# Layer 3's bias table fetched by row gathers inside layer 1, and other orders, banks and buffers at three seams of a four-layer kernel

## The chip, the cores and the metric

The kernel runs on one core of a Trainium2 chip. The core has TensorE (PE in the profile), VectorE (DVE), ScalarE (ACT), GpSimd (POOL) and SyncE (SP), which here only issues DMAs. What counts is the time of one execution on the device in microseconds; several runs of the same program are taken, and the median is given. Every number type in the kernel is 32-bit float, apart from lists of indices.

## What is computed

Four residual layers work on an image batch `x` of shape 4 x 56 x 56 x 256. Each normalises `x` over 32 groups of channels and adds its own result to `x`:

```python
x = x + L0(_gn(x))   # attention of each pixel over its 7 x 7 neighbours, 8 heads of 32
x = x + L1(_gn(x))   # affinity of all 3136 tokens of an image with one another
x = x + L2(_gn(x))   # 7 x 7 neighbourhood attention with bias, dilation 1 and 2
x = x + L3(_gn(x))   # attention in shifted 7 x 7 windows, with bias table and mask
```

The bodies of layers 1 and 3, which the change touches most:

```python
# layer 1, n = 3136 tokens of an image
xn = x / norm(x)
A = exp(5.0 * (xn @ W_adj @ xn.T - rowmax));  A = A * (1 - eye);  A = A / rowsum(A)
diff = rowsum(A) * (x @ W_aff.T + b_aff) - (A @ x) @ W_aff.T
y = layernorm(diff) * gamma + beta;  y = where(y > 0, y, 0.01 * y)
# layer 3, windows of N = 49 tokens, 8 heads
bias = rel_bias_table[rel_index].reshape(N, N, HEADS).transpose(2, 0, 1)
attn = softmax(q @ k.T + bias + mask)      # mask: 0 or -100 by the window's place
out = (attn @ v) @ proj_weight.T + proj_bias
```

`rel_bias_table` has 169 rows of 8 numbers, one for each head; `rel_index` says which row belongs to each of the 49 x 49 pairs of a query and a key.

## The kernel before

The four layers follow one another in one program (`direct_blocks` with `layer0` to `layer3`). `run(l, layer, fixed, kinds)` opens the SBUF pools and the PSUM pool of a layer. In layers 0 and 2 a scheduler decides the order on all engines from the order in which the code gives its steps; in layer 1 the order of PE and DVE is that of the code, in layer 3 that of PE, DVE, ACT and POOL. A layer's stretch in the trace: layer 0 up to about 743 us, layer 1 to 2679, layer 2 to about 3332, layer 3 to the end at 3861.

PSUM tiles have tags. `ps_m` is the bank for projections and other small products (two buffers, in layer 1 one), `ps_s` holds scores, `ps_o` weighted sums, `ps_v` and `ps_t` belong to layer 1.

**The bias table** (`table_steps`, L1955 to L2007). Layer 3 needs for every pair of windows a table of bias plus mask, 98 keys x 8 heads x 98 queries, in four types. It is made inside layer 0's stream, three steps behind each row of attention. `look_up` (seven calls) takes seven queries: a cast of indices (L1974), two comparisons that make one-hot columns (L1977), four PE products with the table (L1981), copies (L1984), seven PE transposes (L1987) and a copy into `base` (L1988). `mask` (four calls) adds the mask's type to `base` (L1994, two halves), takes the exponential for half of the heads (L1996), and stores to the DRAM tensor `m3d` (L1998, eight stores in all). Layer 3 loads all of `m3d` in one piece, `m3l` of 2.46 MB.

**Layer 1** goes through (image, row tile j, range of columns) units. A unit makes scores `ps_s` from `xd` and `xnT` (L1440), exponentials on ACT (L1443), a product on POOL that clears the diagonal (L1445), transposes (L1531), and products into `ps_o` (L1545) and `ps_v` (L1550), of which DVE adds the latter to `acc` (L1472). `scaled(j)` makes `xd`, two POOL instructions (L1433), for a unit two ahead. `finish` makes y of a row tile (L1586 to L1609); its transposes and the addition to x are L1616 and L1624. While image b is worked on, `replace` puts the chunks of image b+1 in place, seven chunks of 512 tokens: token lengths (L1382), values (L1404, in two halves, evacuated by ACT L961 and DVE L959), and a product that spreads the reciprocal lengths (L1414) with which DVE makes `xnT` (L1416). These and L1616 all use `ps_m`, of which layer 1 has one bank.

**Layer 1 to 2.** Layer 2's first row was prepared inside layer 1. Its projections run values first (L979, evacuated by DVE L983), then queries and keys (L952, evacuated by ACT). DVE has layer 1's last tiles ahead of L983.

**Layer 2 to 3.** Layer 2's last additions (L1910) go into `xr` tiles (two buffers), loaded by SP (L1907) and stored by SP (L1913). Layer 3 begins with the values of two rows (L979, L983, stored to `vd` at L987 from one buffer `vt`), then row 0's projections (L952).

**Layer 3** has 32 rows r of 8 windows (four pairs) and two head halves hq, so 64 units (r, hq). `attend_quads` issues for each unit its scores (L1020), the exponentials and masks (L1024 to L1027), then `done` of the unit before (reciprocal L2109, product into `attn` L2111), the fill steps, which are projections of coming rows and the output projection of row r-2, and `products` of the unit before (L1035: first with v, then with ones for the sums). `project_out` multiplies `attn` with `w_p` (L952), adds the bias on ACT (L2131), adds to x on POOL (L2133) and stores. Behind the loop come the last `done`, `products`, `done` and the output projections of the last two rows. A short check of bounds (L2200 to L2208) ends the program.

## Time and profile before

| what | us |
|---|---|
| median of three runs | 3865.4 |
| lowest and highest of them | 3864.78, 3871.85 |
| the profiled execution | 3863.09 |
| its span in the profile | 3861.2 |
| PE without work in the span | 143 |

The rows of section 2 of the page, the span in 40 slices of 96.5 us, show how evenly the engines are used; a digit is the busy share in tenths, in the row PEclk the clock that PE was granted:

```profile
PE   7899999899999999999999999999999999899998
DVE  5676867633445444454444543445577777677775
POOL 3577777611124311242112421124677777555555
PEclk9899999899999999999999999999999999999998
```

The first eight slices are layer 0, the next twenty layer 1, in which PE has nearly all the work and the other engines little; then seven of layer 2 and five of layer 3. A row of the profile's groups gives line, engine, operation, output and input with their shapes and the count, then the busy time and the mean of one in ns, then the idle time of the engine ahead of it and what ended it. A line of the waits gives what an engine waited to do and for whom, with the total in us, the number and the longest. A row of the time line gives the start and the length in us.

### The profile page before, as it was taken

To read this page: it belongs to the slowest core of one execution; us is meant where nothing else is said; L and a number is where in the kernel's file an instruction comes from. 1 tells how busy PE (TensorE), PEld (TensorE's weight loads), DVE (VectorE), ACT (ScalarE), POOL (GpSimd) and SP (SyncE) were. 2 spreads that over 40 slices of the span, in tenths; PEclk is the share of its full clock that TensorE was granted. 3 is DMA by queue.
4 is the path that set the end of the run, shared out by engine and by line. 5 is a ranking of instruction groups with operands and counts; after the bars stand their busy time and mean duration, and the time that the engine had idled before them with its cause. 6 is when DMAs were issued, how large, how long until landed. Compare 5 with 4: busy or idle time off the path is not lost.

```text
span 3861.2 us, 112545 instructions
## 1 busy us (share of the span) xinstructions
PE 3717.8 (96%) x48953; PEld 2499.3 (65%) x48953; DVE 2219.1 (57%) x4232; ACT 1465.1 (38%) x3111; POOL 1761.9 (46%) x1924
## 2 busy tenths in 40 slices
PE   7899999899999999999999999999999999899998
PEld 4465656567777677776777767776666666455554
DVE  5676867633445444454444543445577777677775
ACT  4465656422222222222222222222666666344443
POOL 3577777611124311242112421124677777555555
PEclk9899999899999999999999999999999999999998
DMA  6544443400101000010000100001344444534443
GB/s 215 139 151 143 145 120 113 167 14 12 31 18 33 26 14 21 18 33 26 17 18 18 33 20 10 10 10 51 111 136 129 138 127 118 159 125 136 133 130 96
DMA packets 275650, 305.70 MB, mean 79 GB/s; under 512 B 31302, under 2 KB 266344, under 8 KB 274664
## 3 DMA queue, kind: packets, MB, share of 16 engines
q1 hardware_dynamic: 274858, 298.34, 25.5%
q8 instruction: 386, 6.32, 0.7%
q14 instruction: 118, 0.97, 0.1%
q10 hardware_dynamic: 288, 0.08, 0.0%
HBM read 205.95 MB, written 92.39 MB: 77 GB/s over the span
## 4 chain that ended last, share of the span: by engine, by line
PE 74%; DVE 3%; POOL 1%; issue 1%; ACT 1%; DMA 0%; SPq 0%; DVEq 0%; ACTq 0%; POOLq 0%
PE ps_o L1545 13%; PE ps_s L1440 13%; PE ps_m L952 13%; PE ps_v L1550 12%; PE ps_m L979 4%; PE ps_t L1531 3%; PE ps_o L1097 3%; PE ps_s L1068 3%; PE ps_o L1035 2%; PE ps_m L1404 2%; PE ps_s L1020 1%; PE ps_v L1511 1%; PE ps_o L1515 1%; PE ps_s L1482 1%; PE ps_m L1616 1%
## 5 line engine op out<-in xcount | busy, mean ns | idle before, releaser
L1472 DVE TENSOR_TENSOR acc<-acc,ps_v 128x257 f32<-128x257 f32 x1104 | 463.9, 423 | 785.0 <-PE ps_v L1550 756.4
L1550 PE MATMUL ps_v<-xw,e 128*128 128x257 f32 x2208 | 610.5, 381 | 1.8 <-DVE acc L1472 1.8
L1545 PE MATMUL ps_o<-xw,at 128*128 128x257 f32 x2208 | 609.0, 379 | 0.0
L1440 PE MATMUL ps_s<-xnT,xd 128*128 128x512 f32 (+3 forms) x1344 | 575.7, 551 | 3.9 <-DVE xnT L1416 3.9
L1534 ACT COPY at<-ps_t 128x512 f32<-128x512 f32 (+3 forms) x332 | 170.6, 514 | 957.1 <-PE ps_t L1531 956.9
L1550 PEld LDWEIGHTS ps_v<-xw,e 128*128 128x128 f32 x2208 | 414.2, 189 | 143.4 <-issue 84.1
L1088 POOL TENSOR_TENSOR b<-e 126x336 f32<-126x336 f32 (+5 forms) x512 | 496.9, 991 | 8.9 <-ACT e L1076 1.2
L1545 PEld LDWEIGHTS ps_o<-xw,at 128*128 128x128 f32 x2208 | 419.1, 190 | 60.1
L952 PE MATMUL ps_m<-xn,w_wqkv 128*32 128x392 f32 x4096 | 376.0, 496 | 13.1 <-DVE v L983 7.5
L1433 POOL TENSOR_SCALAR xd<-xnT,vec 128x128 f32<-128x128 f32 x192 | 116.3, 617 | 489.4 <-PE ps_s L1440 489.2
L1079 POOL TENSOR_TENSOR e<-e,m0t 126x672 f32<-126x672 f32 (+3 forms) x128 | 238.8, 1866 | 207.7 <-ACT e L1078 202.7
L1443 ACT ACTIVATE e<-ps_s 128x512 f32<-128x512 f32 x336 | 185.4, 552 | 374.7 <-PE ps_s L1440 367.7
L1440 PEld LDWEIGHTS ps_s<-xnT,xd 128*128 128x128 f32 x1344 | 226.7, 192 | 142.8 <-issue 127.7
L1079 POOL TENSOR_TENSOR e<-e,bias 119x784 f32<-119x784 f32 (+5 forms) x128 | 239.4, 1871 | 155.9 <-ACT e L1078 155.4
L1097 PEld LDWEIGHTS ps_o<-e,vp 124*32 124x32 f32 (+3 forms) x8192 | 199.3, 110 | 105.0 <-issue 82.8
L998 ACT ACTIVATE no<-rs 128x168 f32<-128x168 f32 (+2 forms) x256 | 93.9, 367 | 446.8 <-DVE rs L1875 191.5
L952 PEld LDWEIGHTS ps_m<-xn,w_wqkv 128*32 128x32 f32 x4096 | 123.5, 110 | 189.0 <-issue 129.1
L1875 DVE RECIPROCAL rs<-ps_o 128x196 f32<-128x196 f32 (+2 forms) x128 | 175.7, 1373 | 111.6 <-PE ps_o L1097 107.1
L1097 PE MATMUL ps_o<-e,vp 124*32 124x112 f32 (+3 forms) x8192 | 231.4, 248 | 5.3 <-POOL e L1079 4.6
L1076 ACT ACTIVATE e<-e 126x672 f32<-126x672 f32 (+5 forms) x256 | 219.7, 858 | 17.0 <-DVE e L1075 5.3
L1027 POOL TENSOR_TENSOR e<-e,m3l 98x784 f32<-98x784 f32 x64 | 119.6, 1869 | 205.8 <-ACT e L1024 205.8
L1078 ACT ACTIVATE e<-ps_s 126x672 f32<-126x672 f32 (+5 forms) x256 | 206.3, 806 | 9.1 <-PE ps_s L1068 9.1
(205 smaller groups left out, 6044.1 us busy)
## 6 DMA issues: line engine op xcount, KB each, us to landing
x<-xr SPq DMA_DIRECT2D x64, 392.0 KB
x<-in_x SPq DMA_DIRECT2D x53, 448.0 KB
x<-x SPq DMA_DIRECT2D x60, 392.0 KB
xr<-x SPq DMA_DIRECT2D x60, 392.0 KB
vd<-v SPq DMA_DIRECT2D x72, 256.0 KB
xr<-in_x SPq DMA_DIRECT2D x32, 392.0 KB
xr<-x SPq DMA_DIRECT2D x28, 448.0 KB
x<-xr SPq DMA_DIRECT2D x28, 448.0 KB
```

Source lines behind the costliest of these rows:

```text
L952: nc.tensor.matmul(pm[j * HD:(j + 1) * HD, :n], lhsT=w[:, h, col + j * HD:col + (j + 1) * HD], rhs=rhs(h), start=(h == 0), stop=(h == CC - 1))
L1076: nc.scalar.activation(ev, ev, AF.Exp)
L1078: nc.scalar.activation(ev, sv, AF.Exp)
L1079: nc.gpsimd.tensor_tensor(parts(ev), parts(ev), w["emask"], ALU.mult)
L1088: nc.gpsimd.tensor_tensor(w["b"][a][:nk, :, :2 * nq].rearrange("p h (i c) -> p h i c", i=2), ev[:, :, :, 0, :], ev[:, :, :, 1, :], ALU.add)
L1097: nc.tensor.matmul(w["o"](k, i)[j * HD:(j + 1) * HD], lhsT=ones[:nk, :HD] if k else v(j, u), rhs=w["b"][j // 2][:nk, j % 2, i * nq:(i + 1) ...
L1440: nc.tensor.matmul(s[:, :n], lhsT=xd[j][:, h, :], rhs=xnT[:, h, first * P:last * P], start=(h == 0), stop=(h == CC - 1))
L1443: nc.scalar.activation(e[:, :n], s[:, :n], AF.Exp, scale=5.0)
L1472: nc.vector.tensor_tensor(acc[:, i, :], acc[:, i, :], pv[:, :C + 1], ALU.add)
L1545: nc.tensor.matmul(out[j][:, :C + 1], lhsT=e[:, col(i)] if i == j else at[:, col(i)], rhs=xw[:, i, :], start=(i == j), stop=(i == NB - 1))
L1550: nc.tensor.matmul(pv[:, :C + 1], lhsT=e[:, col(i)], rhs=xw[:, j, :], start=True, stop=True)
L1875: nc.vector.reciprocal(rs.rearrange("p (t c) -> p t c", t=2), pv[:, :, 1, :])
```

## The change

1. The seven look-ups and four masks leave layer 0. In layer 1 a list of indices `idx` (98 rows, one for each of two times 49 keys; 49 columns, one for each query) is loaded, and behind each `scaled(j)` with 0 < j < 20 one gather is issued on POOL: for query q, 98 rows of the table, 8 floats each, to `rows`. Behind each seventh, SP stores them to the DRAM tensor `looked_up`. 49 gathers fall into the first three images.
2. Layer 2 loads `looked_up` and makes the four masks during its row 1 and later rows, at the last unit of a row in the code's order; the scheduler may put them earlier. The table's pools are opened in layer 2.
3. `replace` in layer 1 hands chunks 3, 4 and 5 a function `other_bank` that takes `ps_m` and `ps_v` in turn.
4. `mv` and `rstd` share one tile of the pool `late`.
5. Layer 2's row 0 projects queries, keys, values, in this order; `xr2` has three buffers in place of two; layer 1's late pool is closed earlier.
6. Layer 3: the table is loaded in two halves, `m3a` first and `m3b` behind the weights; `vt3` has two buffers and `xr3` three; two pools change places.
7. In `attend_quads` the sums come ahead of the values, and POOL's product is issued ahead of DVE's addition. The close of layer 3 is written out: products of the last units use `ps_m` banks, output projections the score banks, and the last row's projection is done in two halves of the input channels, the first while the reciprocal of the second is still being made; the bias goes into x by ACT, DVE adds from PSUM, and each half of the channels is stored by itself.

The diff, cut to its core:

```diff
@@ -944,9 +944,9 @@
-def project(w, col, rhs, n):
-    pm = ps_m()
+def project(w, col, rhs, n, pm=None):
+    pm = ps_m() if pm is None else pm
@@ -1011,7 +1011,7 @@
-    def logits(w):
+    def logits(w, between=no_step):
@@ -1022,13 +1022,14 @@
+        nc.gpsimd.tensor_tensor(ev[1], ev[1], w["emask"].to_broadcast([nk, 2, nu * nq]), ALU.mult)
+        between()
-        nc.gpsimd.tensor_tensor(ev[1], ev[1], w["emask"].to_broadcast([nk, 2, nu * nq]), ALU.mult)
-        for k in range(2):
+        for k in (1, 0):
@@ -1045,9 +1046,7 @@
-    done()
-    products(held)
-    held["done"]()
+    return logits, products, held, done
@@ -1295,10 +1294,6 @@
-                steps += table[:3]
-                if len(table) in (1, 2, 3):
-                    steps.append(tables.close)
-                del table[:3]
@@ -1316,9 +1311,6 @@
-    tables = ExitStack()
-    both = [tables.enter_context(tc.tile_pool(name=f"t{n}", bufs=n, side="right", reuse_waits="tile")) for n in (1, 2)]
-    table = table_steps(*both)
@@ -1329,6 +1321,10 @@
+m3d = dram.tile([98, 2, NH, 4, 98], FP, name="m3d")
+looked_up = dram.tile([98, WN, NH], FP, name="looked_up")
@@ -1344,6 +1340,20 @@
+    idx = big.tile([98, WN], I32, name="idx")
+    for w in range(2):
+        nc.sync.dma_start(out=idx[w * WN:(w + 1) * WN], in_=d["relidxT"])
+    def look_up(q):
+        if q % 7 == 0:
+            rows[:] = [pool.tile([98, 7, NH], FP, tag="rows", name="rows", bufs=1)]
+        with tc.issue_after(scaling[-1].ins):
+            nc.gpsimd.indirect_dma_start(out=rows[0][:, q % 7, :], out_offset=None, in_=d["table"][:, :],
+                                         in_offset=bass.IndirectOffsetOnAxis(ap=idx[:, q:q + 1], axis=0))
+        if q % 7 == 6:
+            nc.sync.dma_start(out=looked_up[:, q - 6:q + 1, :], in_=rows[0])
+    looks, scaling, rows = [lambda q=q: look_up(q) for q in range(WN)], [], []
@@ -1430,7 +1440,7 @@
-            nc.gpsimd.tensor_scalar_mul(xd[j][:, h, :], xnT[:, h, j * P:(j + 1) * P], adj[:, h:h + 1])
+            scaling.append(nc.gpsimd.tensor_scalar_mul(xd[j][:, h, :], xnT[:, h, j * P:(j + 1) * P], adj[:, h:h + 1]))
@@ -1593,11 +1603,11 @@
-        mv = pool.tile([P, 2], FP, tag="mv", name="mv1", bufs=7)
+        mv = late.tile([P, 3], FP, tag="mv", name="mv1", bufs=7)
-        rstd = pool.tile([P, 1], FP, tag="rstd", name="rstd", bufs=7)
+        rstd = mv[:, 2:3]
@@ -1688,11 +1698,16 @@
+    banks = iter(range(100))
+    def other_bank():
+        return psum_tile(*(("m", 1), ("v", 2))[next(banks) % 2])
-            (load,), normals[b, c], steps = tokens(b, c)
+            (load,), normals[b, c], steps = tokens(b, c, *([other_bank] if c in (3, 4, 5) else []))
@@ -1720,6 +1735,8 @@
+            if looks and 0 < units[k + 2][1] < 20:
+                looks.pop(0)()
@@ -1903,7 +1920,7 @@
-                box["x"] = pool.tile([P, CC, WC2], FP, tag="xr", name="xr2")
+                box["x"] = pool.tile([P, CC, WC2], FP, tag="xr", name="xr2", bufs=3)
@@ -1930,6 +1947,8 @@
+            if r and table:
+                work[7].append(table.pop(0))
@@ -1937,12 +1956,18 @@
-        for step in project_rows(i):
+        steps = project_rows(i)
+        for step in steps if i else steps[4:] + steps[2:4] + steps[:2]:
+    ends.close()
+    tables = ExitStack()
+    both = [tables.enter_context(tc.tile_pool(name=f"t{n}", bufs=n, side="right", reuse_waits="tile")) for n in (1, 2)]
+    table = table_steps(*both)
+    table.append(tables.close)
@@ -1950,54 +1975,25 @@
-    def look_up(q0):
...
+    found = big.tile([98, WN, NH], FP, name="found")
+    nc.sync.dma_start(out=found, in_=looked_up)
-            nc.vector.tensor_tensor(m[:, :, sl], base, t3[:, ty:ty + 1, sl].to_broadcast([98, NH, WN]), ALU.add)
+            nc.vector.tensor_tensor(m[:, :, sl], found.rearrange("p q h -> p h q"), t3[:, ty:ty + 1, sl].to_broadcast([98, NH, WN]), ALU.add)
-    return [lambda q=q: look_up(q) for q in range(0, WN, NQ)] + [lambda ty=ty: mask(ty) for ty in range(4)]
+    return [lambda ty=ty: mask(ty) for ty in range(4)]
@@ -2015,10 +2011,10 @@
-    def transfer(l, r, x, out):
+    def transfer(l, r, x, out, hs=slice(0, CC)):
-            ends = x[:, :, i0 * S:(i0 + n) * S], tokens_of(l, b, r0 * S, n * S)
+            ends = x[:, hs, i0 * S:(i0 + n) * S], tokens_of(l, b, r0 * S, n * S)[:, hs]
@@ -2029,10 +2025,12 @@
+    m3 = [big.tile([98, NH, 4 * 98], FP, name="m3a")]
+    nc.sync.dma_start(out=m3[0], in_=m3d[:, 0].rearrange("p h w k -> p h (w k)"))
-    m3 = big.tile([98, 2, NH, 4 * 98], FP, name="m3l")
-    nc.sync.dma_start(out=m3, in_=m3d.rearrange("p a h w k -> p a h (w k)"))
+    m3.append(pool.tile([98, NH, 4 * 98], FP, name="m3b", bufs=1))
+    nc.sync.dma_start(out=m3[1], in_=m3d[:, 1].rearrange("p h w k -> p h (w k)"))
@@ -2084,7 +2082,7 @@
-        v = pool.tile([P, 4, C], FP, tag="vt", name="vt3", bufs=1)
+        v = pool.tile([P, 4, C], FP, tag="vt", name="vt3", bufs=2)
@@ -2094,21 +2092,23 @@
-    def quad(r, hq):
+    def quad(r, hq, single=False):
-            if k + u == 0:
-                box["o"] = psum_tile("o", 1, 2)
-            return box["o"][:, k, u * 98:(u + 1) * 98]
+            if not box:
+                pair = None if single else psum_tile("o", 1, 2)
+                for i in (1, 0):
+                    box[i] = ps_m() if single else pair[:, i]
+            return box[k][:, u * 98:(u + 1) * 98]
-            nc.vector.reciprocal(rs, box["o"][:, 1, :WC])
+            nc.vector.reciprocal(rs, box[1][:, :WC])
-            nc.vector.scalar_tensor_tensor(attns[r][:, hq, :], box["o"][:, 0, :WC], 1.0, rs, ALU.mult, ALU.mult,
+            nc.vector.scalar_tensor_tensor(attns[r][:, hq, :], box[0][:, :WC], 1.0, rs, ALU.mult, ALU.mult,
@@ -2116,28 +2116,53 @@
-        mk = m3[:, wr // 7, 4 * hq:4 * hq + 4, :]
+        mk = m3[wr // 7][:, 4 * hq:4 * hq + 4, :]
-        x = pool.tile([P, CC, WC], FP, tag="xr", name="xr3")
+        x = pool.tile([P, CC, WC], FP, tag="xr", name="xr3", bufs=3)
-        def step(m):
-            pm = project(w_p, m * P, lambda h: attns[r][:, h, :], WC)
+        def step(m, pm=None):
+            pm = project(w_p, m * P, lambda h: attns[r][:, h, :], WC, pm)
-        return [lambda m=m: step(m) for m in range(CC)]
+        return [lambda *pm, m=m: step(m, *pm) for m in range(CC)]
+    def last_row(r):
+        x = pool.tile([P, CC, WC], FP, tag="xr", name="xr3", bufs=3)
+        transfer(3, r, x, 0)
+        pms = []
+        def first():
+            pair = psum_tile("o", 1, 2)
+            for m in range(CC):
+                pms.append(pair[:, m, :WC])
+                half(m, 0)
+                nc.scalar.activation(x[:, m, :], x[:, m, :], AF.Identity, bias=bp3[:, m:m + 1])
+        def half(m, h):
+            for j in range(4):
+                nc.tensor.matmul(pms[m][j * HD:(j + 1) * HD], lhsT=w_p[:, h, m * P + j * HD:m * P + (j + 1) * HD],
+                                 rhs=attns[r][:, h, :], start=(h == 0), stop=(h == CC - 1))
+        def second():
+            for m in range(CC):
+                half(m, 1)
+                for w, xv in parts(pms[m], x[:, m, :]):
+                    nc.vector.tensor_tensor(xv, xv, w, ALU.add)
+                transfer(4, r, x, 1, slice(m, m + 1))
+        return first, second
-        for r in range(n):
+        for r in range(n - 1):
@@ -2147,7 +2172,7 @@
-                w = quad(r, hq)
+                w = quad(r, hq, single=(r == n - 2 and hq == 1))
@@ -2159,10 +2184,27 @@
-    attend_quads(pool, stream())
-    for r in range(NIMG * 8 - 2, NIMG * 8):
-        for step in project_out(r):
-            step()
+    logits, products, held, done = attend_quads(pool, stream())
+    r = NIMG * 8 - 1
+    attns[r] = pool.tile([P, CC, WC], FP, tag="attn", name="attn3", bufs=3)
+    u3, u4 = quad(r, 0), quad(r, 1, single=True)
+    out = project_out(r - 2)
+    logits(u3, done)
+    out[0]()
+    products(held)
+    logits(u4, held["done"])
+    products(u3)
+    pair = psum_tile("s1", 1, 2)
+    out[1](pair[:, 0])
+    out = project_out(r - 1)
+    first, second = last_row(r)
+    out[0](pair[:, 1])
+    u3["done"]()
+    products(u4)
+    out[1](psum_tile("s0", 1, 2)[:, 0])
+    u4["done"]()
+    first()
+    second()
@@ -2188,7 +2230,7 @@
-run(3, lambda own: layer3(*own), {E.PE, E.DVE, E.Activation, E.Pool}, range(4))
+run(3, lambda own: layer3(own[1], own[0], *own[2:]), {E.PE, E.DVE, E.Activation, E.Pool}, (1, 0, 2, 3))
@@ -2254,6 +2296,7 @@
+g["relidxT"] = f(np.asarray(i["L3_conv_rel_index"]).reshape(WN, WN).T)
```

More of the change, by code (lines that the diff above doesn't have):

```diff
@@ L1595, in finish @@
             st = pool.tile([P, 6], FP, tag="st", name="st1")
-            mv = pool.tile([P, 2], FP, tag="mv", name="mv1", bufs=7)
+            mv = late.tile([P, 3], FP, tag="mv", name="mv1", bufs=7)
             nc.vector.bn_stats(out=st[:n], in_=y)
-            nc.vector.bn_aggr(out=mv[:n], in_=st[:n])
+            nc.vector.bn_aggr(out=mv[:n, :2], in_=st[:n])
             nc.vector.tensor_scalar_add(mv[:n, 1:2], mv[:n, 1:2], LN_EPS)
-            rstd = pool.tile([P, 1], FP, tag="rstd", name="rstd", bufs=7)
+            rstd = mv[:, 2:3]
             nc.gpsimd.tensor_tensor(rstd[:n], mv[:n, 1:2], mhalf[:n, 0:1], ALU.pow)
@@ L1948, in layer2 @@
             step()
-    m3d = dram.tile([98, 2, NH, 4, 98], FP, name="m3d")
     def table_steps(big, pool):
-        NR, NQ = 169, 7
-        idx = big.tile([P, WN, WN], I32, name="idx")
-        nc.sync.dma_start(out=idx.rearrange("p a b -> p (a b)"), in_=d["relidx"].to_broadcast([P, WN * WN]))
-        row = big.tile([P, 2], I32, name="row")
-        nc.gpsimd.iota(row, pattern=[[P, 2]], base=0, channel_multiplier=1)
-        rowf = big.tile([P, 2], FP, name="rowf")
-        nc.vector.tensor_copy(rowf, row)
-        tab = big.tile([P, 2, NH], FP, name="tab")
-        nc.sync.dma_start(out=tab[:, 0], in_=d["table"][:P])
-        nc.sync.dma_start(out=tab[:NR - P, 1], in_=d["table"][P:])
         t3 = big.tile([98, 4, 98], FP, name="t3")
         nc.sync.dma_start(out=t3, in_=d["c_m3"])
-        base = big.tile([98, NH, WN], FP, name="base")
-        def look_up(q0):
-            idxf = pool.tile([P, NQ, WN], FP, tag="idxf", name="idxf")
-            nc.vector.tensor_copy(idxf, idx[:, q0:q0 + NQ, :])
-            hot = pool.tile([P, 2, NQ * WN], FP, tag="hot", name="hot")
-            for a, n in ((0, P), (1, NR - P)):
-                nc.vector.tensor_scalar(hot[:n, a, :], idxf[:n].rearrange("p q k -> p (q k)"),
-                                        rowf[:n, a:a + 1], None, ALU.is_equal)
-            pb = ps_m()
-            for a, n in ((0, P), (1, NR - P)):
-                nc.tensor.matmul(pb[:NH, :NQ * WN], lhsT=tab[:n, a, :], rhs=hot[:n, a, :], start=(a == 0), stop=(a == 1))
-            tb = pool.tile([NH, NQ, 98], FP, tag="tb", name="tb")
-            for w in range(2):
-                nc.vector.tensor_copy(tb[:, :, w * WN:(w + 1) * WN], pb[:NH, :NQ * WN].rearrange("p (q k) -> p q k", k=WN))
-            pt = ps_m()
-            for q in range(NQ):
-                nc.tensor.transpose(pt[:98, q * NH:(q + 1) * NH], tb[:, q, :], ident[:NH, :NH])
-            nc.vector.tensor_copy(base[:, :, q0:q0 + NQ], pt[:98, :NQ * NH].rearrange("p (q h) -> p h q", h=NH))
+        found = big.tile([98, WN, NH], FP, name="found")
+        nc.sync.dma_start(out=found, in_=looked_up)
         def mask(ty):
```

## The prediction

> **What bounds the kernel now.** I read the page's head and its chain of waits first, then TensorE's waits, then the time line at each place that the change touches.
>
> ```profile
> span 3861.2 us, 112545 instructions
> PE   3717.8 (96%) x48953; PEld 2499.3 (65%) x48953; DVE 2219.1 (57%) x4232; ACT 1465.1 (38%) x3111; POOL 1761.9 (46%) x1924
> PE 74%; DVE 3%; POOL 1%; issue 1%; ACT 1%; DMA 0%; SPq 0%; DVEq 0%; ACTq 0%; POOLq 0%
> ```
>
> TensorE (PE) is busy for 96% of the span and carries the chain; the next engine stands at 57%. Time can be won in three ways only: PE work taken out, PE waits taken out, low-clock stretches avoided. Span minus PE busy is 143 us. The waits (engine, what waited, for whom: total us, times, longest) that lie where the change works:
>
> ```profile
> PE ps_o L1035 <- DVE attn L2111: 9.5, 6, 3.5
> PE ps_m L952 <- DVE v L983: 7.9, 4, 6.9
> PE ps_m L1616 <- DVE xnT L1416: 7.8, 3, 2.6
> PE ps_m L1987 <- DVE tb L1984: 7.5, 4, 3.0
> PE ps_m L979 <- DVE xr L1910: 5.9, 1, 5.9
> PE ps_m L1414 <- DVE xw L959: 2.6, 3, 0.9
> PE ps_m L952 <- DVE vt L983: 2.1, 1, 2.1
> PE ps_m L1404 <- ACT xw L961: 2.0, 3, 0.7
> ```
>
> In order: the close of layer 3, the door from layer 1 to layer 2, layer 1's change of image (three changes: 1616, 1414, 1404), the table look-ups, and the door from layer 2 to layer 3. Together 45 us, nearly a third of all that PE idles.
>
> [...] 32 matmuls of L1035 take 0.89 us at 3821.83 and 1.53 us at 3828.62, behind a wait of 2.90 us. So a wait costs more than its own length.
> [...]
>
> **The change part by part.**
>
> **Layer 0: 7 look-ups and 4 masks leave.** PE's groups in the stretch 60 to 190 us, and the DVE waits between, are all here:
>
> ```profile
> L1981 PE MATMUL ps_m<-hot,tab 128*8 128x343 f32 (+1 forms) x28 | 13.8, 603 | 0.0
> L1987 PE MATMUL ps_m<-ident,tb 8*98 8x8 f32 x49 | 4.3, 208 | 7.5 <-DVE tb L1984 7.5
> ```
>
> 13.8 + 4.3 = 18.1 us of PE work and 7.5 us of waiting: 25.6. Nothing but PE is full there (from 60 to 260 us PE 183.9 of 200, DVE 143, POOL 121, ACT 100), and DVE loses 28 us too (L1977 12.0 by two forms, L1984 6.4, L1994 5.2, L1974 2.9, L1988 1.3). Layer 0 is ordered by the scheduler, and its waits for ACT and DVE may come a little more often once PE catches up: I take 24, bounds 20 to 28 (the clock is granted at 0.91 there, so a little more is possible).
>
> **Layer 1: 49 gathers on POOL.** Each follows a pair of L1433 (2 x 0.617 us). 19 per image, in three images. POOL sat idle 489 us ahead of the 192 L1433, and in the stretch that I looked at 4.94 us between a pair and the next POOL work, the mask L1445 that PE needs next. [...] Behind it in POOL's queue stand L1445, L1586 and the pow L1601. Lower bound 0 (no PE work goes away); upper bound, where a gather outlasts its 4.94 us now and then, 49 x 0.3 = 15. The 7 stores of 22 KB go by SP, nobody waits for them in this layer but the next seventh gather, one tile being used.
>
> **Layer 1: two banks in turn for chunks 3 to 5.** With one ps_m bank the next user waits until the last is evacuated. Alternating with ps_v, L1616 no longer stands behind L1414/L1416 (2.61), values1 not behind the evacuation L961 (0.68), L1414 not behind L959 (0.88): 4.2 per image change, 12.5 for three. The 1.31 of L1440 stays, it needs xnT itself; so does 0.52 for L1624. Against it: ps_v is what L1550 rotates through, and a bank held for an evacuation of 0.6 to 0.7 us can delay an L1550 (0.5 per image, about 1.5). Take 11; bounds 3 (the waits only change bank) and 18 (the four L1440 at 1316.61 took 3.53 instead of 1.88 us, low clock, and that goes as well).
>
> **Layer 1 to 2: row 0's projections run queries, keys, values.**
>
> ```profile
> 2679.53 2.80 PE L979 MATMUL ps_m<-w_wqkv,xn 128*32 128x256 f32 x48
> 2689.18 7.01 PE L952 MATMUL ps_m<-xn,w_wqkv 128*32 128x392 f32 x64 [6.85 <-DVE v L983]
> ```
>
> L983 stands on DVE behind the tail of layer 1's y (L1604, L1609) and comes only at 2688.45. The four L952 groups need ACT alone, which is free by 2683.5, so their 7.01 us fill the hole, then 2.80 of L979, and L983 comes at about 2690.2: a wait of some 0.9 is left. Take 6; bounds 4 and 7.
>
> **Masks at layer 2's head.** 8 L1994 of 0.697 us now read the gathered rows with a stride, 4 exponentials, 8 stores (2.5 MB), and loads of t3, the rows and m3a (1.23 MB) on SP. About half falls into 5.5 us in which DVE is idle at 2712; the rest delays a L1075 or L983 by up to 1.2 us each. Take -2; bounds 0 and -4 (a strided read is in no trace; twice 0.697 is the upper end I allow).
>
> **Layer 2 to 3.**
>
> ```profile
> 3336.94 1.16 DVE L1910 SCALAR_TENSOR_TENSOR xr<-ps_m,vec,xr 128x392 f32<-128x392 f32 x2 [5.77 <-issue]
> 3338.15 8.18 PE L979 MATMUL ps_m<-w_wqkv,xn 128*32 128x256 f32 x96 [5.89 <-DVE xr L1910]
> 3348.43 3.83 PE L952 MATMUL ps_m<-xn,w_wqkv 128*32 128x392 f32 x44 [2.10 <-DVE vt L983]
> ```
>
> DVE waits for the last xr, which SP asks for at 3330.71, behind the store that frees its buffer and in the wake of the 2.46 MB table load issued at 3322.65. Three buffers let it load a row earlier, half of the table is in place since layer 2, and two vt buffers take the 2.10 (L983 waited for the store of vt). The 96 L979 should take 5.6 us (32 take 1.91) and took 8.18: 2.6 of low clock go too. 5.89 + 2.10 + 2.6 = 10.6; a rest of about 1.5 stays. Take 9; bounds 6 and 11. The other half of the table now loads beside the v gather: late by up to 8 us it harms nobody.
>
> **Steady layer 3.** Sums before values, POOL's multiply issued before DVE's add, other tile homes: PE is busy 472 of 473 us from 3350 to 3823. Cost 0.
>
> **The close of layer 3.** From 3823.3 PE works, waits 2.90, 2.22 and 3.47 us for L2111, and runs half of its work at low clock; last, 64 L952 (two rows of projection):
>
> ```profile
> 3828.62 1.53 PE L1035 MATMUL ps_o<-e,v 98*32 98x98 f32 x32 [2.90 <-DVE attn L2111]
> 3837.89 0.89 PE L1035 MATMUL ps_o<-e,v 98*32 98x98 f32 x32 [2.22 <-DVE attn L2111]
> 3843.42 1.53 PE L1035 MATMUL ps_o<-e,v 98*32 98x98 f32 x32 [3.47 <-DVE attn L2111]
> 3846.00 6.96 PE L952 MATMUL ps_m<-attn,w_wp 128*32 128x392 f32 x64
> ```
>
> Laying out the new order with full-clock durations (L1020 0.95, L1035 0.87 a half, L952 1.52 a half, L2109 2.60, L2111 0.57): scores of (31,0) end at 3824.2, DVE has (30,0) by 3826.5 and adds its mask by 3827.5, scores of (31,1) end 3828.5, products of (31,0) 3830.2, projections fill to 3833.2, products of (31,1) run 3833.2 to 3835.0, one more projection, L2109 and L2111 for (31,1) end at 3838.1 while PE does the early half of the last projection, the late half is done at 3839.7, the last DVE add about 3841, against 3855.1 for the last L2133 now. That is 14. The check at the end (L2200 to L2208) now stands behind the last adds instead of beside them, and 7.1 us lay between it and the end of the span: 3 us go back. Take 11; bounds 5 (PE waits again for reciprocals, low clock) and 14.
>
> **Sum.** 24 + 11 + 6 - 2 + 9 + 11 = 59. The profiled execution took 3863.1 us (span 3861.2), 2.3 below the median of 3865.4; 3863.1 - 59 = 3804, and on the median's footing 3806. All good ends: 28 + 18 + 7 + 11 + 14 = 78, 3787. All bad ends: 20 + 3 + 4 - 4 + 6 + 5 = 34, 3831, or 3846 with gathers at 15.
>
> **Rivals.**
> - Layer 0 isn't set by PE where the look-ups stood: L1068 waits for L1075 and L952 for kE already (7.8 and 7.6 us), so its neighbours inherit the time and 24 becomes 5: 3825. For it: the look-ups were placed by a scheduler that could fill holes. Against: the look-ups caused waits themselves, no engine but PE is above 72% there.
> - The bank swap only shifts the waits to L1550, and the close goes on waiting for reciprocals: 11 and 11 become 3 and 5: 3820.
> - Slower: the gathers hold POOL. Everything else brings 59, so they must cost 49 x 1.36 us or more on PE's path to be slower by 0.2%. With 4.94 us of cover a gather would have to hold POOL about 6.3 us[...]; at 8 us it would be 49 x 3.06 = 150 lost, 3896. For it: nothing in the trace shows such a DMA[...]. Against: POOL's idle time is wide.
>
> **How the numbers follow.** This kernel's measurement tells 0.2% (7.7 us) from no change. Chances: forecast 0.64 (3788 to 3816), layer 0 not set by PE 0.14, swap and close moved only 0.13, gathers slower 0.06, gains just eaten up 0.03. 8 in 10 lie from 3788 to 3832. Faster 0.91, same 0.03, slower 0.06.
>
> **What would show it.** L1987's wait gone and layer 0 ending near 718 instead of 743; at each image change only 1.31 and 0.52 left; no wait over 2 us at the first L979 of layer 2 or at layer 3's start; the stretch from 3823 to the end about 11 us shorter; POOL's gathers each under 5 us and no new wait of PE for e or xd in layer 1. Wrong: L1440 or L1545 waiting for POOL, L1550 for L1472 for longer, layer 0's L1068 and L1097 waits up by over 10 us, or layer 2's first 60 us longer.

## The result and the profile after

The changed kernel takes 3800.4 us in the median of six runs (3789.3 to 3803.0), against 3865.4 us for the kernel before (six runs): a ratio of 0.9823, with a 95% interval of 0.9807 to 0.984. That is 65 us less, 6 us below the forecast of 3806 and inside its range. The sum was right; four of its terms were not, two too small and two too large.

The page of the changed kernel, its head and its chain of waits (the profiled execution took 3789.3 us, the shortest of the six):

```profile
span 3787.5 us, 112437 instructions
PE 3672.9 (97%) x48876; PEld 2486.9 (66%) x48876; DVE 2201.7 (58%) x4195; ACT 1463.2 (39%) x3111; POOL 1811.6 (48%) x1966
PE 87%; DVE 7%; POOL 2%; ACT 2%; issue 1%; DMA 1%; SPq 0%; DVEq 0%; ACTq 0%; POOLq 0%
```

PE is busy 44.9 us less (3717.8 to 3672.9) and idle 28.8 us less. Only 18.1 us of PE work left the program. So some 27 us of the busy time that vanished, an estimate from these two numbers, are the same matmuls at a higher clock (the mean granted over the span rose from 0.985 to 0.994): this is the first thing that the prediction undervalued. POOL is 50 us busier: the gathers.

PE's waits in the changed kernel (what waited, for whom: total us, times, longest). Line numbers of layer 1 are up by ten, L1075 is now L1074, L1035 is L1036:

```profile
PE ps_s L1067 <- DVE e L1074: 12.8, 13, 2.4
PE ps_s L1450 <- DVE xnT L1426: 3.9, 3, 1.3
PE ps_m L1036 <- ACT pr L2131: 2.6, 1, 2.6
PE ps_o L2152 <- DVE xr L2159: 2.6, 1, 2.6
PE ps_m L979 <- DVE v L983: 2.4, 1, 2.4
PE ps_v L1560 <- DVE xnT L1426: 2.2, 3, 0.7
PE ps_m L952 <- ACT kE L1828: 1.4, 1, 1.4
PE ps_m L979 <- DVE vt L983: 0.6, 1, 0.6
```

Of the eight waits shown before, the largest of L1035, L1616, L1987, L979 for xr, L1414 and L1404 are gone; the 6.9 us for the values (v) shrank to 2.4 us, the 2.1 us for vt to 0.6 us. The 3.9 us of L1450 stay as foreseen. New are: 5.2 us in the close (L1036 for L2131, L2152 for L2159), the 2.4 us of L1067 and the 1.4 us for kE in layer 2's head, and, over the three image changes, 2.2 us of L1560 and 2.3 us more of L1626 waiting for xr (3.8 us in place of 1.5).

To see where the time went, the span is cut at seven matmuls that both kernels have: the first product with ones of layer 1, the first with `xdr`, layer 2's first projection, the first statistics in layer 2 (L914), its last product (L1097), layer 3's first scores (L1020), and the scores of unit (31,0). A second execution of the changed kernel (from the experiments) stands beside the first:

| stretch | before | after | after, again | forecast of the difference |
|---|---|---|---|---|
| layer 0 | 744.4 | 703.3 | 706.0 | -24 |
| start of layer 1 | 53.0 | 48.9 | 53.4 | 0 |
| rest of layer 1 | 1882.2 | 1866.6 | 1866.6 | -11 |
| layer 2, head | 53.8 | 56.6 | 57.5 | -4 (order -6, masks +2) |
| layer 2, rest | 592.3 | 592.6 | 594.2 | 0 |
| layer 2 to 3 | 28.2 | 18.0 | 18.0 | -9 |
| layer 3 | 469.5 | 469.7 | 469.7 | 0 |
| close, to the span's end | 37.9 | 31.7 | 31.2 | -11 |
| span | 3861.2 | 3787.5 | 3796.6 | -59 |

The differences of the first execution add up to -73.7, those of the second to -64.6. Between the two executions, 4.5 us lie in the start of layer 1, where the order is the same, and the rest in layers 0 and 2; the start of layer 1 took 53.0 us before and 53.4 us in the second execution, so its 4 us in the first are no effect of the change. They are the clock: it was granted at 0.90 in this stretch of the first execution and at 0.82 in the second, as in the kernel before (0.82), while PE was idle for 4.5 us in all three. The times of whole runs show the same: the two short ones of the six (3789.3 and 3789.9 us) have a mean granted clock of 0.994 and 0.995, the other four (3799.0 to 3803.0 us) of 0.991 and 0.992.

**Layer 2's head** is the stretch that went the wrong way. DVE in the changed kernel, from the time line (start, length, operation, idle time ahead of it and what ended it):

```profile
2647.84 3.21 DVE L1990 TENSOR_TENSOR m<-found,t 98x392 f32<-98x392 f32 x4 [0.73 <-DMA found<-looked_up]
...
2661.91 1.62 DVE L1990 TENSOR_TENSOR m<-found,t 98x392 f32<-98x392 f32 x2 [4.71 <-DMA m3d<-m]
2663.45 0.96 DVE L1074 TENSOR_TENSOR e<-ps_s,bias 85x784 f32<-85x784 f32 x1
```

and PE at the same place:

```profile
2664.47 1.96 PE L1067 MATMUL ps_s<-q,kI 32*90 32x84 f32 x32 [2.38 <-DVE e L1074]
2666.36 2.84 PE L952 MATMUL ps_m<-xn,w_wqkv 128*32 128x392 f32 x16
2668.97 1.53 PE L1096 MATMUL ps_o<-e,vp 85*32 85x98 f32 x32
```

The masks have two buffers. The third mask's addition waits until the first mask is stored, and DVE stands for 4.71 us with the scores' addition L1074 behind it in its queue. PE waits 2.38 us for that addition, and what follows runs at half clock (granted from 2664.4 to 2671.2 us). The same three groups in the kernel before:

```profile
2725.03 0.88 PE L1068 MATMUL ps_s<-q,kI 32*90 32x84 f32 x32
2725.84 1.52 PE L952 MATMUL ps_m<-xn,w_wqkv 128*32 128x392 f32 x16
2727.18 0.86 PE L1097 MATMUL ps_o<-e,vp 85*32 85x98 f32 x32
```

Wait and low clock make 2.38 + 1.08 + 1.32 + 0.67 = 5.5 us that go back to buffers that were missing.

**The close.** PE in the changed kernel:

```profile
3761.49 0.89 PE L1036 MATMUL ps_m<-e,v 98*32 98x98 f32 x32 [2.64 <-ACT pr L2131]
...
3766.86 1.52 PE L952 MATMUL ps_s<-attn,w_wp 128*32 128x392 f32 x16 [0.79 <-ACT pr L2131]
...
3776.01 0.86 PE L2152 MATMUL ps_o<-attn,w_wp 128*32 128x392 f32 x8 [2.60 <-DVE xr L2159]
```

The reciprocals are no longer waited for. In their place PE waits for ACT's evacuation and for DVE's last addition, and the clock holds (0.86 to 0.89 for a half of L1036). From the scores of (31,0) to the end of the span PE is idle for 16.6 us in both kernels; its busy time for the same matmuls fell from 21.2 to 15.1 us. So what the new close gained is clock, not idle time. At the very end, from the matmul of the check (n_safe) to the end of the span, 9.65 us pass, before 7.45.

### The profile page after: what moved, and what is told of

Its sections match the earlier page's. It is cut to its first block, busy times and chain, and to the rows that moved or that the text cites. A ratio compares the mean times of both kernels' runs of the same rounds, so it can differ in the third digit from the quotient of the medians.

```text
span 3787.5 us, 112437 instructions
## 1 busy us (share of the span) xinstructions
PE 3672.9 (97%) x48876; PEld 2486.9 (66%) x48876; DVE 2201.7 (58%) x4195; ACT 1463.2 (39%) x3111; POOL 1811.6 (48%) x1966
## 4 chain that ended last, share of the span: by engine, by line
PE 87%; DVE 7%; POOL 2%; ACT 2%; issue 1%; DMA 1%; SPq 0%; DVEq 0%; ACTq 0%; POOLq 0%
PE ps_m L952 17%; PE ps_o L1555 14%; PE ps_s L1450 13%; PE ps_v L1560 13%; PE ps_m L979 7%; PE ps_o L1096 5%; PE ps_s L1067 5%; PE ps_t L1541 3%; PE ps_o L1036 2%; PE ps_s L1020 1%; PE ps_m L1414 1%; POOL b L1087 1%; DVE e L1074 1%; DVE rs L1247 1%; PE ps_v L1521 1%
## 5 line engine op out<-in xcount | busy, mean ns | idle before, releaser
L1560 PE MATMUL ps_v<-xw,e 128*128 128x257 f32 x2208 | 611.3, 381 | 3.4 <-DVE xnT L1426 2.2
L1555 PE MATMUL ps_o<-xw,at 128*128 128x257 f32 x2208 | 609.2, 380 | 0.0
L1450 PE MATMUL ps_s<-xnT,xd 128*128 128x512 f32 (+3 forms) x1344 | 571.6, 548 | 3.9 <-DVE xnT L1426 3.9
L1560 PEld LDWEIGHTS ps_v<-xw,e 128*128 128x128 f32 x2208 | 414.4, 190 | 143.6 <-issue 83.1
L1555 PEld LDWEIGHTS ps_o<-xw,at 128*128 128x128 f32 x2208 | 419.9, 190 | 59.2
L952 PE MATMUL ps_m<-xn,w_wqkv 128*32 128x392 f32 x4096 | 376.2, 496 | 6.0 <-ACT gst L917 3.9
L1450 PEld LDWEIGHTS ps_s<-xnT,xd 128*128 128x128 f32 x1344 | 225.8, 191 | 141.1 <-issue 126.0
L952 PEld LDWEIGHTS ps_m<-xn,w_wqkv 128*32 128x32 f32 x4096 | 124.4, 110 | 180.0 <-issue 128.1
L1075 ACT ACTIVATE e<-e 126x672 f32<-126x672 f32 (+5 forms) x256 | 219.6, 858 | 13.3 <-DVE e L1074 1.1
L979 PE MATMUL ps_m<-w_wqkv,xn 128*32 128x256 f32 x3136 | 197.8, 383 | 3.1 <-DVE v L983 2.4
```

What stands on the lines that cost most here:

```text
L952: nc.tensor.matmul(pm[j * HD:(j + 1) * HD, :n], lhsT=w[:, h, col + j * HD:col + (j + 1) * HD], rhs=rhs(h), start=(h == 0), stop=(h == CC - 1))
L979: nc.tensor.matmul(pm[i:i + HD, j * C:(j + 1) * C], lhsT=xn[:, h, first + i:first + i + HD], rhs=w[:, h, :], start=(h == 0), stop=(h == CC ...
L1075: nc.scalar.activation(ev, ev, AF.Exp)
L1450: nc.tensor.matmul(s[:, :n], lhsT=xd[j][:, h, :], rhs=xnT[:, h, first * P:last * P], start=(h == 0), stop=(h == CC - 1))
L1555: nc.tensor.matmul(out[j][:, :C + 1], lhsT=e[:, col(i)] if i == j else at[:, col(i)], rhs=xw[:, i, :], start=(i == j), stop=(i == NB - 1))
L1560: nc.tensor.matmul(pv[:, :C + 1], lhsT=e[:, col(i)], rhs=xw[:, j, :], start=True, stop=True)
```

## The experiments

Twelve runs were made. A median is of four runs in the same round as the kernel before, unless a single run is named; for the stretches the landmarks of the table above are used.

### The changed kernel once more

> The changed kernel once more, for the spread between executions and as the measure for the other three. Theory 1 (the gain of layer 0 beyond its PE work and its wait is the clock that the waits behind the look-ups had taken away): layer 0 again lasts about 703 us and its clock from 60 to 200 us is granted at 0.98 or more; where this execution is 10 us longer than the profiled one of the changed kernel (3787.5), the difference lies in stretches of low clock at the starts of layers and not in any wait of fixed place. Rival (the gain of layer 0 is a lucky execution): layer 0 lasts 710 us or more.

Median 3804.4 us (3798.4 to 3807.4), ratio 0.9842 (0.9825 to 0.9858); layer 0 706.0 us. So the gain of layer 0 is no lucky execution: in ten executions of kernels with this layer 0, these and the ones below, it lasted 703.2 to 707.8 us. The spread lies in stretches of low clock that come or don't: the start of layer 1 takes 48.5 to 50.6 us or 52.3 to 53.7 us, whatever the kernel, and the close as it was changed takes 31.2 to 31.7 us in five executions, 34.7 and 36.4 us in two.

This bears on how the medians below can be read. The second set of runs of the changed kernel has granted clocks of 0.989 to 0.993, and its median lies 9 to 12 us above those of three edits in the same round, although one of them (the close) shortens its stretch by only 2 us. So an edit that is worth less than some 10 us is better priced by its stretch in the profiled execution than by the medians.

### Layer 0: the look-ups out, the masks out, the waits out

The kernel before without its look-ups:

```diff
-        def look_up(q0):
...
+        nc.vector.memset(base, 0.0)
...
-        return [lambda q=q: look_up(q) for q in range(0, WN, NQ)] + [lambda ty=ty: mask(ty) for ty in range(4)]
+        return [lambda ty=ty: mask(ty) for ty in range(4)]
```

> The kernel before without its look-ups (base is zero, so the position bias is missing); the masks and their stores stay in layer 0. Theory 1 (the look-ups alone make the 38 us that layer 0 lost): layer 0 ends near 706 us instead of 744. Rival (the masks and their eight stores in layer 0 have a part in it): it ends between 712 and 725 us.

Single run 3849.6 us (the kernel before beside it 3865.9), layer 0 723.4 us: 21 of the 38 us. Theory 1 falls, and the number is the rival's. The masks now find `base` ready at once and are put forward, to the head of layer 0, and there the same thing happens as in layer 2 after the change. DVE in this kernel:

```profile
62.04 0.57 DVE L1978 TENSOR_TENSOR m<-base,t 98x392 f32<-98x392 f32 x1 [5.84 <-DMA m3d<-m]
...
65.19 1.28 DVE L983 TENSOR_TENSOR v<-ps_m,bc 128x512 f32<-128x512 f32 x2
```

and PE:

```profile
65.93 3.21 PE L952 MATMUL ps_m<-xn,w_wk 128*32 128x448 f32 x16 [5.08 <-DVE v L983]
```

The third mask waits 5.84 us for a store and PE 5.08 us for what stands behind it. This run doesn't price the look-ups alone; it shows that masks with two buffers cost time wherever they are put ahead of something that PE needs.

The kernel before with its look-ups and without the masks' arithmetic:

```diff
         def mask(ty):
-            m = pool.tile([98, NH, 98], FP, tag="m3", name="m3")
...
-            nc.scalar.activation(mv, mv, AF.Exp)
             for pair in [3] if ty % 2 else range(3):
-                nc.sync.dma_start(out=m3d[:, ty // 2, :, pair, :], in_=m)
+                nc.sync.dma_start(out=m3d[:, ty // 2, :, pair, :], in_=t3[:, ty:ty + 1, :].to_broadcast([98, NH, 98]))
```

> The kernel before with its look-ups, but without the masks' additions and exponentials in layer 0 (the stores take the mask constants alone, so the position bias is missing from the result). Theory 1 (what layer 0 lost beyond the 21 us that go with the look-ups alone is the masks: their third addition waits on VectorE for a store, and scores and keys stand behind it): layer 0 shrinks from 744 to 725-730 us, and PE's wait of 3.0 us for kE at 169.7 us and of 2.7 us for e at 186 us go. Rival (look-ups and masks share one low-clock stretch, which either alone would end): it shrinks to 715 us or less, more than the rest. Second rival (masks cost little in layer 0): 738 us or more.

Single run 3859.8 us (before: median 3862.8); layer 0 740.7 us, so 3.7 us, no more than ten executions of one layer 0 differ by (4.6 us): the second rival holds. PE's wait for kE fell from 3.0 to 1.0 us, that for e of 2.7 us stayed. Theory 1 falls: what the look-ups alone don't explain isn't the masks' arithmetic in its old place.

The kernel before with each look-up cut in two, so that other work lies between the products and the transposes:

```diff
+        def turn(q0):
+            tb = tbs[q0]
             pt = ps_m()
             for q in range(NQ):
                 nc.tensor.transpose(pt[:98, q * NH:(q + 1) * NH], tb[:, q, :], ident[:NH, :NH])
...
+        return [first[0]] + [f for a, b in zip(first[1:], turns) for f in (a, b)] + [turns[-1]] + ...
...
-                    steps += table[:3]
+                    steps += table[:5]
```

> The kernel before with each look-up cut in two: the transposes of one come behind the first products of the next, five steps in a row instead of three. No PE work leaves. Theory 1 (PE's waits behind the look-ups cost about 7.5 us themselves and some 13 us of low clock after them): layer 0 shrinks from 744 to 722-730 us, L1987's waits fall under 2 us, and the clock from 60 to 200 us rises from 0.82-0.91 to 0.97 or more. Rival (the low clock has nothing to do with those waits): L1987's waits go, layer 0 shrinks by the 7.5 us at most, and the clock stays under 0.92.

Single run 3853.4 us, layer 0 733.7 us: 10.7 us less, between the theories. What it shows is finer than what was asked. Up to the row in which the order is the same again (265 us in the kernel before), PE was idle 34.5 us in the kernel before and 35.1 us here; no PE work left, and yet the stretch is 10.8 us shorter. The table of stretches of the kernel before (from and to, length, busy us and count of PE, PEld, DVE, ACT and POOL, then the clock granted to PE, the DMA share, GB/s):

```profile
80.00:90.00 10.00, 7.49 (x82) 3.32 (x80) 9.76 (x15) 2.63 (x6) 4.97 (x4) 0.71 0.60 188
90.00:100.00 10.00, 10.00 (x78) 3.69 (x81) 6.79 (x10) 4.09 (x10) 4.92 (x3) 0.61 0.01 2
...
110.00:120.00 10.00, 8.02 (x159) 3.97 (x151) 9.90 (x16) 3.41 (x6) 7.10 (x6) 0.91 0.63 206
120.00:130.00 10.00, 10.00 (x89) 5.19 (x90) 5.22 (x12) 2.30 (x4) 3.34 (x3) 0.50 0.23 68
```

and of the split kernel:

```profile
80.00:90.00 10.00, 8.34 (x184) 5.04 (x182) 9.95 (x18) 2.19 (x4) 7.15 (x6) 1.00 0.57 185
90.00:100.00 10.00, 8.05 (x132) 3.83 (x133) 5.37 (x9) 6.73 (x18) 4.41 (x3) 1.00 0.01 2
...
110.00:120.00 10.00, 9.34 (x204) 5.67 (x206) 9.93 (x18) 2.19 (x4) 7.46 (x6) 1.00 0.59 190
120.00:130.00 10.00, 10.00 (x200) 5.22 (x192) 5.34 (x9) 6.39 (x18) 4.32 (x3) 1.00 0.17 56
```

Between 120 and 130 us PE is busy all the time in both kernels, and does 89 matmuls in one and 200 in the other: the clock stands at 0.50 and at 1.00. In the kernel before, waits of 2.1 and 2.0 us stand ahead of these stretches; in the split kernel none over 1.8 us. Up to that row, the kernel before has 37.5 us at half clock, 30.7 us of them behind three waits for a look-up (2.1, 2.0 and 3.0 us); the split kernel has 13.7 us, the changed kernel none. Half of 37.5 - 13.7 is 11.9 us, an estimate of the PE work that the low clock took, beside the 10.8 us measured. So the waits behind the look-ups cost more in clock (half of 30.7 us, an estimate of 15 us) than their own length (7.1 us), and with the sum of idle time unchanged it is the long single waits that did it. That is theory 1 in its mechanism; its size (14 to 22 us) was too large because other waits of up to 1.85 us came in, one of which, at 141 us, was followed by 6.8 us at half clock. The edit also puts five steps into a row instead of three; what that does by itself was not run.

With this the 40.8 us that the stretch up to 265 us lost in the changed kernel can be laid out: 16.0 us of L1981 and L1987 (by the time that they alone fill), 9.4 us of idle time, and the rest, some 15 us, the same L952, L979, L1068 and L1097 at a higher clock.

### Layer 1: one bank again, and four gathers for one

```diff
-                (load,), normals[b, c], steps = tokens(b, c, *([other_bank] if c in (3, 4, 5) else []))
+                (load,), normals[b, c], steps = tokens(b, c)
```

> Layer 1 with all chunks on its one ps_m bank again, the rest as in the changed kernel. Theory 1 (the 15.6 us that layer 1 lost from its first attention unit to its end are the banks' alone): this stretch is 1882 us again instead of 1866.6, with waits of 2.6, 0.7 and 0.9 us at each of three image changes (12.5 us), and the rest as low clock behind them: L1450 at 3.5 instead of 1.9 us for four. Rival (part of the gain comes from mv and rstd in one tile, or from the gathers' place): the stretch is 1871 to 1878 us.

Single run 3818.5 us; layer 1 behind its start 1883.8 us. Theory 1 holds: the banks alone make the whole gain of layer 1. The four executions with the kernel before's layer 1 took 1882.2 to 1884.0 us there, so the gathers, which this run still has, cost nothing that can be seen. PE's waits in this kernel:

```profile
PE ps_m L1626 <- DVE xnT L1426: 8.4, 3, 2.9
PE ps_m L1424 <- DVE xw L959: 2.6, 3, 0.9
PE ps_m L1414 <- ACT xw L961: 2.0, 3, 0.7
```

13.0 us of waits, of which 2.2 us come back in the changed kernel as L1560 waiting for xnT and 2.3 us as L1626 waiting for xr. In all PE is idle for 10.8 us less; the rest of the 17.1 us, some 6 us, is put down to the clock: the kernel before has three half-clock stretches of 3.41 us in its layer 1, at 1316, 1798 and 2241 us, and the changed kernel none (granted 1.00 from 755 to 2610 us).

```diff
+                for extra in more:
+                    nc.gpsimd.indirect_dma_start(out=extra[:, q % 7, :], out_offset=None, in_=d["table"][:, :],
+                                                 in_offset=bass.IndirectOffsetOnAxis(ap=idx[:, q:q + 1], axis=0))
```

> Each of layer 1's 49 gathers is issued four times, three of them into tiles that nobody reads. Theory 1 (POOL is free for 4.9 us behind a scaling, and a gather holds it for 1.06 us): four take 4.2 us, layer 1 from its first unit to its end stays at 1866.6 us within 2 us. Rival (gathers cost PE time whenever POOL's queue is longer): 49 times 3 gathers at 0.3 us or more on the path, 44 us or more.

Single run 3808.4 us; layer 1 behind its start 1871.3 us: 4.6 us for 147 gathers more, 0.03 us for each. More than theory 1 allowed, and a tenth of the rival. (The whole run is longer than that: its close took 36.4 us.) In the changed kernel POOL's row for the gathers, between 755 and 2218 us:

```profile
L1351 POOL DMA_INDIRECT rows<-in_table,idx x47 | 49.8, 1060 | 9.6 <-issue 9.6
```

A gather holds POOL for 1.06 us, and its rows have landed 2.4 us (median) after the issue; nothing on PE waits for it. The first of PE's attention products that wait for POOL appear with four gathers (the products into `ps_o`, L1555 of the changed kernel, for e): 1.3 us in each of two images.

### Layer 2's head: masks without arithmetic, later, or with more buffers

In the changed kernel the masks' additions and exponentials are left out, by the same edit as in the kernel before:

> The masks' eight additions on VectorE and four exponentials on ScalarE are left out (the stores take the mask constants alone, so the position bias is missing from the result); all loads and stores stay. Theory 1 (the mask additions stand at the head of VectorE's queue, the third waits for the store of the first, and the scores' additions stand behind it): the stretch from layer 2's first projection to the first projection behind the third row's statistics shrinks from 60.2 to about 52.5 us, and the whole by 7 to 8 us. Rival (the stores and the load of half the table crowd the DMA queues of layer 2's head): the stretch stays at 59 to 60 us and the whole within 1 us of the changed kernel.

Median 3792.1 us (3791.5 to 3792.7), ratio 0.9807 (0.9791 to 0.9823); the head 50.0 us instead of 57.5. Theory 1 holds for the head, though all stores and loads stay: it costs 7.5 us because of the arithmetic and its place in DVE's queue.

```diff
-                if r and table:
-                    work[7].append(table.pop(0))
+                if r > 8 and table:
+                    def behind(step):
+                        with tc.issue_after(added[0].ins):
+                            step()
+                    work[7].append(lambda step=table.pop(0): behind(step) if table else step())
```

> The four masks are made from row 9 of layer 2 on, one in a row, each behind an addition of the row before; all else as in the changed kernel. Theory 1: layer 2's head shrinks by the same 7 to 8 us, and nothing of it comes back later, since VectorE has 28% of idle time there. Rival (mask work costs its time wherever it stands, some 7 us of VectorE): the head shrinks, the middle of layer 2 grows by 5 us or more, and the whole is within 2 us of the changed kernel.

Median 3794.3 us (3792.8 to 3794.4), ratio 0.9812 (0.9795 to 0.9828); the head 49.6 us. The third image's stretch of layer 2, where the masks now stand, grew from 155.5 to 158.5 us. So of 7.9 us saved 3 come back: the truth lies between the theory and its rival. In the two runs named last below, which have the same late masks, that stretch took 160.6 and 159.6 us, so up to 5 us come back. The median lies 10.1 us below that of the changed kernel in the same round, more than the edit explains.

```diff
-            m = pool.tile([98, NH, 98], FP, tag="m3", name="m3")
+            m = pool.tile([98, NH, 98], FP, tag="m3", name="m3", bufs=4)
```

> The changed kernel with four buffers for the masks in place of two, so that no mask addition waits for a store. Theory 1 (the wait for the store, 4.7 us on VectorE with the scores' addition behind it, is what layer 2's head pays for): the stretch from layer 2's first projection to the statistics behind its third row shrinks from 57 to 51-53 us. Rival (it is the eight additions and four exponentials themselves, wherever they wait): it stays at 56 us or more.

Median 3793.1 us (3789.1 to 3797.1), ratio 0.9822 (0.9806 to 0.9839); the head 51.2 us. DVE in this kernel makes all eight additions in one piece:

```profile
2647.74 6.41 DVE L1990 TENSOR_TENSOR m<-found,t 98x392 f32<-98x392 f32 x8 [0.78 <-DMA found<-looked_up]
2654.52 1.09 DVE L1074 TENSOR_TENSOR e<-ps_s,bias 95x896 f32<-95x896 f32 x1 [0.37 <-PE ps_s L1067]
```

Theory 1 holds: the wait for the store was 5 to 6 us of the head, the eight additions themselves about 1. The edit is one number in one line. For the whole kernel a gain is not shown: the ratio is that of the changed kernel (0.9823), and the rest of layer 2 took 596.7 us in the profiled execution, against 592.6 and 594.2. An addition with the strided read takes 0.86 us in the changed kernel, the median of its eight, against 0.56 us with the contiguous read in the kernel before; the 0.70 us of the prediction is a mean that holds one addition of 1.50 us.

### The close

```diff
-        logits(u3, done)
-        out[0]()
+        logits(u3, lambda: (done(), out[0]()))
...
                 for m in range(CC):
                     half(m, 1)
+                for m in range(CC):
                     for w, xv in parts(pms[m], x[:, m, :]):
```

> In the close of layer 3 the output projection of row 29 is given to ScalarE ahead of the second exponential of unit (31,0), so that its bank is free earlier, and the last row's two late halves are multiplied before VectorE adds either. Theory 1 (PE's waits of 2.64 us for L2131 and of 2.60 us for L2159 lie on the path to the end): both go, and the span shrinks by 4 to 5 us. Rival (the end is set by the check of bounds, whose sum stands ahead of the last additions on VectorE and waits for POOL): the wait of 2.64 goes and the span shrinks by 2 to 3 us. Second rival (the end is set by SyncE's last stores): less than 1 us.

Median 3795.3 us (3793.8 to 3797.4), ratio 0.9817 (0.98 to 0.9833). The close, from the scores of (31,0) to the end, takes 29.4 us instead of 31.7 or 31.2. Both waits are gone, and the gain is 2 us: the first rival holds. Two later runs with the same close took 29.3 and 29.4 us. Where the wait of 2.64 us stayed, it was followed by a half-clock stretch in two of seven executions, and these are the ones whose close took 34.7 and 36.4 us. DVE at the end of this kernel:

```profile
3778.99 0.29 DVE L2242 TENSOR_REDUCE bounds<-watch 128x1 f32<-128x128 f32 x1
3780.57 0.56 DVE L2242 TENSOR_REDUCE bounds<-watch 128x1 f32<-128x392 f32 x1 [1.30 <-POOL watch L993]
...
3781.87 1.29 DVE L2160 TENSOR_TENSOR xr<-xr,ps_o 128x343 f32<-128x343 f32 x6
3783.53 0.15 DVE L2250 TENSOR_SCALAR flag<-n_safe 1x1 int32<-1x1 f32 x1 [0.37 <-PE n_safe L2249]
```

The last additions were free to start when PE was done, but stand behind the check's sum, which waits for POOL.

Late masks and the edited close together, and the same with the check's sums moved behind the last additions:

> Masks from row 9 of layer 2 on, and the close with ScalarE's early turn and the two late halves multiplied first. If the two gains add: 3794.3 - 2.3 = 3792 us in the median. If the close's gain is only a shift of the wait, 3794.

> As the one before, and the sums of the check of bounds behind the last additions to x on VectorE instead of ahead of them. Theory (the last store and the check's flag are both released earlier, the flag by some 1 us): 1 us less than the one before. Rival (nine microseconds follow the flag whatever stands ahead, and the sums now begin later): no less, or up to 1 us more.

Medians 3788.2 us (3786.7 to 3792.2), ratio 0.9805 (0.9789 to 0.9821), and 3789.0 us (3785.7 to 3794.9), ratio 0.9806 (0.9789 to 0.9822). The first is below both numbers that were expected (3792 and 3794). Moving the check brought nothing that these runs can tell: its rival holds. The first of the two has the lowest ratio of all, but its interval overlaps that of the changed kernel (0.9807 to 0.984). In its profiled execution the head is 7.8 us and the close 1.9 us shorter than in the second execution of the changed kernel, and the rest of layer 2 is 3.7 us longer. That it is better is likely; the runs don't settle by how much.

## Why the prediction was right, and where its steps were not

Direction, size and range were right: 65 us in the median against 59. But the steps erred by +15 and +5 us one way and by about 5 us each the other way, and the sum was lucky in that.

- **Layer 0, forecast 24 (bounds 20 to 28), measured 38 to 41.** The term that was mis-sized is the clock, put down as "a little more is possible". The prediction concluded from one pair of readings (32 L1035 in 1.53 us behind a wait of 2.90 us, in 0.89 us elsewhere) that a wait costs more than its own length, had seen a granted clock of 0.91 from 60 to 260 us, and still counted the waits at their own length. The split kernel showed it: with as much idle time in shorter pieces, 10.8 us less.
- **The rival for layer 0 (other waits inherit the time)** fell: idle time shrank by 9.4 us in the stretch up to 265 us.
- **Gathers, forecast 0, measured 0.** The price in POOL time was 1.06 us, inside the 4.94 us of idle time that the prediction had read behind a scaling (from issue to landing a gather took 2.4 us). That it would fit was the author's estimate: the kernel before has no gather from which to read it. The slower rival would have needed 6.3 us, six times as much; even four gathers in place of one cost only 4.6 us in all, and none of the 49 held POOL for more than 1.22 us. One sum of that rival is off: 150 us lost beside the other gains end near 3956 us, not at 3896.
- **Banks, forecast 11 (3 to 18), measured 15.6.** The waits named were the right ones, and their values too. What came back at other waits was 4.5 us, 2.2 of them at ps_v (estimated at 1.5). The low clock at the image changes (three stretches of 3.41 us before, none after), counted only in the upper bound, went with them.
- **Layer 1 to 2, forecast 6 (4 to 7), measured 4.7** to the end of row 0 and 1's values (18.3 to 13.6 us): L983 was waited for 2.4 us instead of the 0.9 us left over.
- **Masks, forecast -2 (0 to -4), measured -7.5.** This is the step that failed, and a sign that the prediction had named for being wrong, a longer start of layer 2, did come. "About half falls into 5.5 us in which DVE is idle" asked only whether DVE had time for the additions. It didn't ask what the additions wait for: with two buffers the third needs a store to have landed. The kernel before showed it, in its DVE time line, and the working passed it by:

```profile
165.85 0.80 DVE L1994 TENSOR_TENSOR m<-base,t 98x392 f32<-98x392 f32 x1 [2.51 <-DMA m3d<-m]
```

  The step was moved together with its wait, from a place where it cost 3.7 us (one run, within the spread) to one where it costs 7.5.
- **Layer 2 to 3, forecast 9 (6 to 11), measured 10.2.** Right in each part: the 96 L979 of layer 3's start wait 0.63 us in all, and each 48 of them take 2.8 us, at a granted clock of 1.00.
- **Steady layer 3, forecast 0, measured +0.2.**
- **The close, forecast 11 (5 to 14), measured 6.1 and 6.7.** The order laid out in the prediction had PE and DVE in it, but not ACT: L2131 stands on ACT behind the second exponential L1028, which waits for DVE (2.64 us). Nor did it ask when the second half of a PSUM pair is free while DVE reads the first (2.60 us). And 2.2 us went between the check and the end of the span. PE idles as long as before (16.6 us); the 6 us are low clock that no longer comes: 17.1 us at half clock between 3828.5 and 3849.1 us before, and a clock of 1.00 from 3750.0 to 3777.1 us after.

## What to carry to other kernels

Price a wait of TensorE at more than its length where it is two microseconds or longer: at 19 of the 25 such waits that began at full clock in the traces of the kernel before and of the changed kernel, the clock fell to half, for 3.41 us or more, and cutting long waits into shorter ones brought 10.8 us here without any work removed. The low clock differs from execution to execution (the start of layer 1 was granted 0.90 in one of the changed kernel and 0.82 in another), so compare stretches, and their granted clock, before a few microseconds are put down to an edit. When a step is moved, take its own waits along: look up in the profile what ended the idle time ahead of it, and count the buffers that it needs in its new place. And lay out a rewritten ending for every engine that stands between two matmuls, not for the two busiest.

## What the runs showed of the hardware

- In the traces of the kernel before and of the changed kernel the granted clock is either full or half. Their half-clock stretches last 3.41, 6.83, 10.24 or 13.65 us, one to four times 3.41 us (the last of each trace runs past the end of the span), and within a trace their beginnings lie whole multiples of 3.41 us apart. A stretch of 3.41 us takes about 1.7 us of PE work (an estimate: half of its length). One can also come with no wait of PE ahead of it, as at 719 us in the changed kernel, where PE had worked without a gap of 0.1 us since 704 us.
- Of the 25 waits of PE of 2 us or more in these two traces that began at full clock, 19 had a half-clock stretch begin during the wait or within 3.4 us of its end; of the 32 from 1 to 2 us, 3 (those of 1.98, 1.31 and 1.32 us). Length alone doesn't settle it: in the kernel before, waits of 2.11 and 1.98 us were followed by 13.65 us at half clock each, two of 2.99 and 3.01 us by 3.41 us each, and of three of 2.61 us one by 3.41 us and two by none; a wait of 2.17 us at 354 us brought a drop and one of 2.18 us at 524 us none.
- An indirect DMA of 98 rows of 32 bytes held POOL for 1.06 us (1.03 to 1.22) and had landed after 2.4 us (median; 7.3 at most); 49 of them in layer 1 cost PE nothing that could be seen.
- From the check's flag to the end of the span 9.3 us pass in the changed kernel and 7.1 us in the kernel before; in nine other executions with the changed close or its edits it was 8.7 to 9.5 us eight times and 11.6 us once. Why isn't shown; moving the last stores and the check by a microsecond or two brought nothing that can be seen (medians of 3789.0 and 3788.2 us).
